# A two-layer graph attention kernel: in the first gather, product 1 is copied from one PSUM bank to another and product 2 is added onto the copy

## The chip, the cores and the metric

The kernel runs on one core of one Trainium2 chip. The metric is the device time of one execution in microseconds; lower is better. A core has five engines with their own instruction queues: TensorE (PE, matmuls), VectorE (DVE), ScalarE (ACT), GpSimd (POOL) and SyncE (SP, which here issues DMAs). Each works through its queue in order and waits for others by semaphores. Matmuls write to PSUM, which has eight banks; ACT and DVE read them out.

## What is computed

Layer norm and ReLU on x (32 batches of 512 nodes by 512 features), then two graph attention layers, then x is added back. Cut to its core:

```
h = relu(layernorm(x))
def gat_layer(x, mask, W, a_src, a_dst, bias, concat):
    xl = (x @ W).reshape(B, N, H, F)
    e = leaky_relu(asrc[:, :, None, :] + adst[:, None, :, :], 0.2)
    e = where(mask, e, -1e9)
    attn = softmax(e, axis=1)
    out = einsum('bsdh,bshf->bdhf', attn, xl)    # the gather
    ...
h = elu(gat_layer(h, mask, W1, ..., concat=True))     # 4 heads of 256 features
h = gat_layer(h, mask, W2, ..., concat=False)         # 1 head of 512
return x + h
```

The gather of the first layer is, for each batch and each of four heads, a product of a 512 x 512 attention matrix `p` with a 512 x 256 block of `xl`, in fp32.

## The kernel before

**Work.** Each batch goes through these stages: loads, norm and transposes (`load`, `norm`, `norm_turn`), masks (`masks`), the first projection (`project1`), the attention weights of four heads (`Soft.first`, `Soft.second`), the first gather (`gather1`), elu (`elu`), the second projection (`project2`), weights of the single head, and the second gather (`gather2`), after which the output is stored. The main loop (L1698) interleaves the stages of batches i, i+1 and i+2: gather of heads 0 and 1 of batch i+1, first half of the projection of batch i+2, gather of heads 2 and 3, the rest of the projection, second gather of batch i, second projection of batch i+1. The first batch is done with plain products (`gather1_plain`, four tiles at a time), before the loop.

**Seven products.** Nearly all matrix products are done as 2 x 2 blocks with Strassen-Winograd's seven block products instead of eight. For this, DVE first makes sums of blocks: for the gather, `sums1` (L1380) makes s1, s2, s4 from `xl` (tile `hs`) and t1, t2 from `p` (tiles `t`), and changes one block of each in place. `BLOCK` (L1152) says to which block of the result each product first goes, and `ACC` (L1154) in which PSUM bank of the unit it is summed: products 1, 6, 7, 4 share bank "a" one after another, 5 and 3 share "b", and 2 has "g" for itself. The result's blocks come from partial sums: block (0,0) is 1 + 2, block (0,1) is 1 + 6 + 5 + 3, and so on. After each product the bank is read out: products 1, 4, 5 and 6 by ACT (`activation`, Identity with scale -1 and the bias), which writes a block of `h1` (tile `h` in the profile), products 2, 7 and 3 by DVE, which subtracts the bank from the block that is already in `h1`. So block (0,0) is written by ACT from product 1 and then changed by DVE with product 2. Product 6 is added by PE onto bank "a" after product 1 has been read out. After products 3 and 4, `elu` (L1343) runs on the half that is then complete: an exponential on ACT (`xr<-h`), then one operation on DVE (`h<-xr,h`).

**Order of the gather.** `PAIRS_OF` (L1428) gives the order of PE's products for two heads at a time: 1, 2, 6, 5, 7, 3, 4, each for the first head and then for the second. The gather of the last batch has an order of its own, `SINGLY` (L1431). Product 5 needs s1 and t1, product 6 needs s2 and t2, products 1, 2, 4 and 7 need blocks of `p` and `xl`.

**Banks.** `Banks` (L46) hands out the eight PSUM banks at build time, first in, first out. With `kept`, `take` gives only a bank that some matmul has written at least that wide, and returns None when there is none; this is for banks that ACT fills and PE then adds onto (`start=False`). The second projection (`sevens`, with a bias `b_sb`) and a small product of the first batch's successor (`forked` in `project1`) do this already: `mm<-b_sb` and `mm<-mm` in the profile.

**What sets the order.** Every operation is entered in a list of jobs (`Program.add`) with a cost and the keys it reads and writes. PE's order is the order of entry. For the other four engines a planner (`Program.order` at L375, `better` at L440, `Run`) simulates the whole program with these costs, looks for places where PE would wait, and changes priorities until it finds fewer. So when a cost, an order or a dependency changes anywhere, the order of DVE, ACT, POOL and SP can change everywhere, from the first instruction on. One job of `gather1` is one product: two matmuls of 128 x 256, each of which is two records in the trace.

All ACT operations of the kernel have line L646 in the profile, all DVE operations L649, most SP DMAs L652, the POOL DMAs L657 and all matmuls L663, since helpers record them; the tiles tell them apart: `mm` are the PSUM banks, `p` the attention weights, `l` the logits on their way to the softmax denominators, `ht` the transposed input, `hs` and `t` the sums of blocks, `stats` the norm's statistics.

Of the kernel before, what the change touches and what calls it, by code (L numbers as in the profile page):

```python
# [15 lines left out]
AF = mybir.ActivationFunctionType  # L16
# [496 lines left out]
def tile_gat(  # L513
# [55 lines left out]
    def tiles(name, n, shape, dtype=F32, pool=sbuf):  # L569
        return [pool.tile(shape, dtype, name=f"{name}{i}") for i in range(n)]  # L570
# [49 lines left out]
    banks = Banks(tiles("mm", 8, [P, 512], F32, psum))  # L620
# [18 lines left out]
    def give_p(pk):  # L639
        if pk[0] == "p":  # L640
            ps_.give(pk)
# [3 lines left out]
    def act(cost, reads, writes, *a, **k):  # L645
        prog.add("ACT", cost, reads, writes, lambda: nc.scalar.activation(*a, **k))  # L646

    def dve(cost, reads, writes, f, *a, **k):
        prog.add("DVE", cost, reads, writes, lambda: f(*a, **k))  # L649
# [10 lines left out]
    def pe(reads, writes, n, calls):  # L660
        def emit():
            for f, a, k in calls:
                f(*a, **k)  # L663

        prog.add("PE", n, reads, writes, emit)
# [440 lines left out]
    M = N // 2  # L1106
# [236 lines left out]
    def elu(g):  # L1343

        keys = [("h1", g, r) for r in range(2)]
        ek, e = xrs.take()
        act(0.62, keys, [ek], e, h1[:, g, :], AF.Exp, bias=-1.0)
        dve(
            0.65, [*keys, ek], keys, nc.vector.scalar_tensor_tensor,
            h1[:, g, :], e, 1.0, h1[:, g, :], op0=OP.min, op1=OP.max,  # L1350
        )
        xrs.give(ek)
# [27 lines left out]
    def sums1(h, pk, p, apart):  # L1380


        def a_block(i, j):
            return (
                xl[:, 2 * j : 2 * j + 2, h, 2 + i * P : 2 + (i + 1) * P],
                [("xl", 2 * j + k, h, i) for k in range(2)],
            )

        def b_block(r, c):
            return (  # L1390
                p[:, 2 * r : 2 * r + 2, c * M : (c + 1) * M], p_keys(pk, (2 * r, 2 * r + 1), (c,))
            )

        a11, a12, a21, a22 = (a_block(i, j) for i in range(2) for j in range(2))
        b11, b12, b21, b22 = (b_block(r, c) for r in range(2) for c in range(2))
        k = KQ + h % 2
        s1, s2 = (
            (hs[:, i, k, :].rearrange("p (k f) -> p k f", f=P), [("hs", i, k)]) for i in range(2)
        )
        s4 = s2  # L1400
        if apart:
            s4 = (hs4[:, h % 2, :].rearrange("p (k f) -> p k f", f=P), [("hs", 2, h % 2)])
        t1, t2 = (
            (t.rearrange("p (k f) -> p k f", f=M), [q]) for q, t in (ts_.take() for _ in range(2))
        )

        def op(cost, f, to, u, v):
            dve(cost, u[1] + v[1], to[1], f, to[0], u[0], v[0])

        add, sub = nc.vector.tensor_add, nc.vector.tensor_sub  # L1410
        op(0.34, add, s1, a21, a22)
        op(0.59, sub, t1, b12, b11)
        op(0.34, sub, s2, s1, a11)
        op(0.59, sub, t2, b22, t1)
        op(0.34, sub, a21, a11, a21)
        op(0.59, sub, b12, b22, b12)
        if apart:
            op(0.34, sub, s4, a12, s2)
        return (
            {1: a11, 2: a12, 3: s4, 4: a22, 5: s1, 6: s2, 7: a21},  # L1420
            {1: b11, 2: b21, 3: b22, 4: b21, 5: t1, 6: t2, 7: b12},
            lambda: op(0.59, sub, b21, b21, t2),
            (lambda: None) if apart else (lambda: op(0.34, sub, s4, a12, s2)),
        )
# [1 line left out]


    PAIRS_OF = tuple(  # L1428
        tuple((h + i, n) for n in (1, 2, 6, 5, 7, 3, 4) for i in range(2)) for h in (0, 2)
    )  # L1430
    SINGLY = (  # L1431
        (0, 1), (0, 5), (0, 2), (0, 6), (0, 3), (1, 1), (0, 7), (1, 5), (1, 2), (0, 4), (1, 6), (1, 3),
        (2, 1), (1, 7), (2, 5), (2, 2), (1, 4), (2, 6), (2, 3), (3, 1), (2, 7), (3, 5), (3, 2), (2, 4),
        (3, 6), (3, 3), (3, 7), (3, 4),
    )

    def gather1(soft, order):

        blocks, bank = {}, {}
        ahead = {h for h, n in order[:2]}  # L1440
        for h in sorted(ahead):
            blocks[h] = sums1(h, *soft.p[h], order is SINGLY)
        for h, n in order:
            if h not in blocks:
                blocks[h] = sums1(h, *soft.p[h], order is SINGLY)
            left, right, late, fourth = blocks[h]
            if n == 4:
                late()
            acc = ACC[n]
            first = n in (1, 2, 5)  # L1450
            if first:
                bank[h, acc] = banks.take(M)
            bk, bt = bank[h, acc]
            ps = bt[:, :M]
            (a, akeys), (w, wkeys) = left[n], right[n]
            pe(
                akeys + wkeys, [bk], KQ * M / 593,
                [
                    (mm, (ps, a[:, k, :], w[:, k, :]),
                     dict(start=(first and k == 0), stop=(k == KQ - 1), skip_group_check=True))  # L1460
                    for k in range(KQ)
                ],
            )
            if n == 6:
                fourth()
            r, c = BLOCK[n - 1]
            g = h * FPH + r
            to, key = h1[:, g, c * M : (c + 1) * M], ("h1", g, c)
            if n in (1, 4, 5, 6):
                act(  # L1470
                    COPY, [bk, "b1"], [key], to, ps, AF.Identity, bias=b1_sb[:, g : g + 1], scale=-1.0,
                )
            else:
                dve(ADD, [bk, key], [key], nc.vector.tensor_sub, to, to, ps)
            if n in (2, 3, 4):
                banks.give(bk)
            if n in (5, 6):
                ts_.give(right[n][1][0])

            if n in (3, 4):  # L1480
                elu(g)
            if n == 4:
                give_p(soft.p.pop(h)[0])
                yield h
# [213 lines left out]
    for i in range(B - 1):  # L1698
# [3 lines left out]
        if last:  # L1702
            for h in gather1(s, SINGLY):
                if h < 2:
                    s.second(h + 2)
                if h == 0:
                    S2[i] = second_layer(i)
                if h == 2:
                    S2[i].second(0)
        else:  # L1710
            run(gather1_plain(s, (0, 1)) if i < PLAIN else gather1(s, PAIRS_OF[0]))
            s.second(2)
            s.second(3)
            S2[i] = second_layer(i)
            S2[i].second(0)
        if front:
# [6 lines left out]
            n = S1[i + 2] = Soft(i + 2, 1, scores_1)  # L1723
# [3 lines left out]
        if not last:  # L1727
            run(gather1_plain(s, (2, 3)) if i < PLAIN else gather1(s, PAIRS_OF[1]))
# [68 lines left out]
```

## Time and profile before

| what | value |
|---|---|
| median of 3 runs | 2760.99 us (2758.34 to 2761.75) |
| the profiled execution | 2761.27 us, its span 2759.5 us |
| mean granted PE clock | 0.999 |
| ACT busy, of the span | 81%, 4751 records |
| POOL busy, of the span | 12%, 356 records |
| DMA | 502.10 MB, mean 182 GB/s |

The span runs from the first to the last instruction on the core; the execution's own time is 1.8 us longer. A profile line of a group reads: line, engine, operation, output tile <- input tiles, shapes, count, then busy us in total, mean ns of one, then the idle time of the engine just before these instructions and what ended it. Durations of instructions that follow each other on one engine overlap: a DVE operation of 128 x 256 has a duration of 0.42 us, and the next one starts some 0.33 us after it. In timelines the columns are start (us from the span's start), duration, engine, line, operation, tiles, shapes and count; consecutive alike instructions are merged. In the table of stretches the columns are the stretch, its length, then busy time and count of PE, PE's weight loads, DVE, ACT and POOL, the granted PE clock, the DMA share and GB/s.

### The profile page before, as it was taken

To read this page: it belongs to the slowest core of one execution; us is meant where nothing else is said; L and a number is where in the kernel's file an instruction comes from. 1 tells how busy PE (TensorE), PEld (TensorE's weight loads), DVE (VectorE), ACT (ScalarE), POOL (GpSimd) and SP (SyncE) were. 2 spreads that over 40 slices of the span, in tenths; PEclk is the share of its full clock that TensorE was granted. 3 is DMA by queue.
4 is the path that set the end of the run, shared out by engine and by line. 5 is a ranking of instruction groups with operands and counts; after the bars stand their busy time and mean duration, and the time that the engine had idled before them with its cause. 6 is when DMAs were issued, how large, how long until landed. Compare 5 with 4: busy or idle time off the path is not lost.

```text
span 2759.5 us, 41946 instructions
## 1 busy us (share of the span) xinstructions
PE 2735.3 (99%) x12490; PEld 2365.6 (86%) x12490; DVE 2627.4 (95%) x6864; ACT 2244.0 (81%) x4751; POOL 323.8 (12%) x356
## 2 busy tenths in 40 slices
PE   7999999999999999999999999999999999999999
PEld 6688888888888888888888888888888888888887
DVE  8999999999999999999999999999999999999996
ACT  5978788888888788887889888888888898888883
POOL 0110111101111011101011110111111110101110
PEclk9999999999999999999999999999999999999999
DMA  8657766667666676776786667767667776668663
GB/s 233 176 153 181 206 178 172 182 179 202 180 184 178 177 184 188 187 183 169 187 204 184 172 178 191 190 184 188 171 180 181 200 189 165 181 183 210 165 172 107
DMA packets 375862, 502.10 MB, mean 182 GB/s; under 512 B 222804, under 2 KB 227668, under 8 KB 375636
## 3 DMA queue, kind: packets, MB, share of 16 engines
q1 hardware_dynamic: 329844, 332.68, 43.7%
q0 software_dynamic: 45792, 166.74, 24.8%
q8 instruction: 101, 1.65, 0.2%
q14 instruction: 125, 1.02, 0.1%
HBM read 316.41 MB, written 51.31 MB: 133 GB/s over the span
## 4 chain that ended last, share of the span: by engine, by line
PE 92%; DVE 3%; DMA 2%; ACT 2%; issue 1%; SPq 0%; DVEq 0%; ACTq 0%
PE mm L663 92%; ACT l L646 1%; DVE p L649 1%; DMA as<-das 0%; DMA adj<-in_adj_dram 0%; DVE h L649 0%; DMA rr<-drr 0%; DVE hs L649 0%; DMA p<-dm 0%; DVE w_sb L649 0%; ACT p L646 0%; DVE l L649 0%; DVE xr L649 0%; DVE t L649 0%; ACT xl L646 0%
## 5 line engine op out<-in xcount | busy, mean ns | idle before, releaser
L663 PE MATMUL mm<-w_sb,hs 128*128 128x257 f32 (+2 forms) x3032 | 697.5, 381 | 5.1 <-DVE hs L649 4.5
L663 PEld LDWEIGHTS mm<-w_sb,hs 128*128 128x128 f32 x3032 | 575.5, 190 | 91.4 <-DVE hs L649 6.1
L657 POOL DMA_DIRECT2D p<-dm x314 | 275.6, 887 | 2261.3 <-DVE p L649 1081.8
L646 ACT ACTIVATE l<-l,low 128x512 f32<-128x512 f32 x640 | 457.4, 717 | 16.0 <-DVE low L649 14.7
L663 PE MATMUL mm<-w_sb,h 128*128 128x257 f32 x2056 | 468.1, 379 | 0.7 <-ACT xl L646 0.7
L663 PE MATMUL mm<-p,xl 128*128 128x256 f32 (+1 forms) x1984 | 465.7, 382 | 0.0
L649 DVE SCALAR_TENSOR_TENSOR p<-rr,z 128x512 f32<-128x512 f32 (+1 forms) x636 | 454.7, 745 | 0.6 <-DMA rr<-drr 0.5
L646 ACT ACTIVATE l<-as,z 128x512 f32<-128x512 f32 x640 | 438.4, 714 | 17.2 <-DMA as<-das 16.6
L663 PEld LDWEIGHTS mm<-w_sb,h 128*128 128x128 f32 x2056 | 389.2, 189 | 59.1 <-ACT xl L646 1.1
L649 DVE CUSTOM_DVE_ANT_1 l<-l,mt 128x512 f32<-128x512 f32 x640 | 427.0, 686 | 7.3 <-ACT l L646 6.4
L663 PEld LDWEIGHTS mm<-p,xl 128*128 128x128 f32 x1984 | 376.8, 190 | 58.6 <-issue 6.9
L646 ACT ACTIVATE p<-p,z 128x512 f32<-128x512 f32 (+1 forms) x636 | 419.0, 716 | 9.6 <-DVE p L649 8.4
L663 PE MATMUL mm<-w_sb,ht 128*128 128x258 f32 x1802 | 421.3, 382 | 3.0 <-DVE xl L649 2.3
L646 ACT ACTIVATE h<-mm,b_sb 128x256 f32<-128x256 f32 (+1 forms) x504 | 232.3, 474 | 204.1 <-PE mm L663 201.8
L663 PEld LDWEIGHTS mm<-w_sb,ht 128*128 128x128 f32 x1802 | 340.1, 190 | 58.6 <-DVE xl L649 7.8
L646 ACT ACTIVATE xl<-mm 128x258 f32<-128x258 f32 (+2 forms) x686 | 253.4, 379 | 96.5 <-PE mm L663 93.3
L649 DVE TENSOR_TENSOR xl<-xl,mm 128x258 f32<-128x258 f32 (+1 forms) x526 | 215.4, 421 | 34.0 <-PE mm L663 29.0
L663 PE MATMUL mm<-t,hs 128*128 128x256 f32 x992 | 225.2, 379 | 0.0
L663 PEld LDWEIGHTS mm<-t,hs 128*128 128x128 f32 x992 | 188.5, 190 | 25.6
L646 ACT ACTIVATE xr<-h 128x512 f32<-128x512 f32 x256 | 158.4, 627 | 53.6 <-DVE h L649 52.6
L649 DVE TENSOR_TENSOR t<-mm,t 128x256 f32<-128x256 f32 (+1 forms) x424 | 172.3, 420 | 13.3 <-PE mm L663 11.9
L663 PE MATMUL mm<-xl,p 128*128 128x256 f32 (+1 forms) x752 | 179.4, 387 | 0.0
(132 smaller groups left out, 3475.1 us busy)
## 6 DMA issues: line engine op xcount, KB each, us to landing
p<-dm POOLq DMA_DIRECT2D x314, 512.0 KB, 5.9
rr<-drr SPq DMA_DIRECT2D x159, 512.0 KB
x<-in_x_dram SPq DMA_DIRECT2D x129, 256.0 KB
adj<-in_adj_dram SPq DMA_DIRECT2D x128, 256.0 KB
as<-das SPq DMA_DIRECT2D x64, 512.0 KB
t<-in_x_dram SPq DMA_DIRECT2D x124, 256.0 KB
out_dram<-t SPq DMA_DIRECT2D x124, 256.0 KB
dm<-m SPq DMA_DIRECT2D x64, 256.0 KB
```

The source lines that it names most:

```text
L646: prog.add("ACT", cost, reads, writes, lambda: nc.scalar.activation(*a, **k))
L649: prog.add("DVE", cost, reads, writes, lambda: f(*a, **k))
L657: lambda: nc.gpsimd.dma_start(to, at, accum_op=OP.add), size,
L663: f(*a, **k)
```

## The change

In `gather1`, for all batches but the first and the last (30 batches, 4 heads, 120 times), product 1 is no longer written to `h1`. ACT copies it from bank "a" to a bank taken for it, which becomes bank "g" (`fork`, a plain Copy). Product 2 is then accumulated by PE onto this copy (`start=False`), and the sum of both is written to `h1` by one ACT operation with scale and bias. The DVE subtraction of product 2 is gone. The order of the products becomes 1, 5, 6, 2, 7, 3, 4. The last batch's gather (`SINGLY`) is as before. If no bank can be had, the old way is taken.

```diff
     PAIRS_OF = tuple(
-        tuple((h + i, n) for n in (1, 2, 6, 5, 7, 3, 4) for i in range(2)) for h in (0, 2)
+        tuple((h + i, n) for n in (1, 5, 6, 2, 7, 3, 4) for i in range(2)) for h in (0, 2)
     )
...
             acc = ACC[n]
-            first = n in (1, 2, 5)
+            first = n in (1, 5) or n == 2 and (h, "g") not in bank
             if first:
                 bank[h, acc] = banks.take(M)
...
             to, key = h1[:, g, c * M : (c + 1) * M], ("h1", g, c)
-            if n in (1, 4, 5, 6):
+            fork = banks.take(M, M) if n == 1 and order is not SINGLY else None
+            if fork:
+                bank[h, "g"] = fork
+                act(0.29, [bk], [fork[0]], fork[1][:, :M], ps, AF.Copy)
+            elif n in (1, 4, 5, 6) or n == 2 and not first:
                 act(
                     COPY, [bk, "b1"], [key], to, ps, AF.Identity, bias=b1_sb[:, g : g + 1], scale=-1.0,
                 )
```

## The prediction

> **What bounds the kernel now.** I read the engine totals first, then the chain that ended last.
>
> ```profile
> PE 2735.3 (99%) x12490; PEld 2365.6 (86%) x12490; DVE 2627.4 (95%) x6864; ACT 2244.0 (81%) x4751; POOL 323.8 (12%) x356
> PE 92%; DVE 3%; DMA 2%; ACT 2%; issue 1%; SPq 0%; DVEq 0%; ACTq 0%
> ```
>
> TensorE (PE) is busy for 2735.3 of 2759.5 us and is 92% of the chain. VectorE (DVE) comes close behind, ScalarE (ACT) has room. The change takes DVE work away, so the first question is how much PE ever waits. The waits of PE:
>
> ```profile
> PE mm L663 <- ACT x L646: 10.6, 2, 10.3
> PE mm L663 <- DVE hs L649: 4.8, 3, 4.3
> PE mm L663 <- DVE xl L649: 2.3, 3, 1.3
> PE mm L663 <- ACT xl L646: 1.2, 2, 0.7
> ```
>
> Columns: total us, times, longest. 10.3 us are the first load and norm, before any matmul; 4.3 are one wait near 48 us. Then busy time by stretch (span and PE's busy time stand first):
>
> ```profile
> 100.00:2600.00 2500.00, 2497.19 (x11481) 2174.38 (x11480) 2404.97 (x6198) 2077.09 (x4392) 298.48 (x323) 1.00 0.69 182
> 2600.00:2700.00 100.00, 97.98 (x448) 84.10 (x447) 96.77 (x234) 82.37 (x179) 12.10 (x14) 1.00 0.61 164
> ```
>
> The 60 changed gathers lie between 135 and 2633 us, all but the last before 2606. From 100 to 2600 us PE idles 2500 - 2497.19 = 2.8 us. So in its own place the change cannot win much more than 2.8 us, 0.1%, whatever it does for DVE.
>
> **The change, part by part.** Counted in the two programs as built: PE has 6261 matmuls in both, SP and POOL the same numbers of instructions, so no DMA is added or removed. DVE loses 120 subtractions `h<-h,mm`; ACT gains 120 copies `mm<-mm` (30 batches x 4 heads). The rows:
>
> ```profile
> L649 DVE TENSOR_TENSOR h<-h,mm 128x256 f32<-128x256 f32 x372 | 151.5, 419 | 1.8 <-PE mm L663 0.5
> L646 ACT ACTIVATE h<-mm,b_sb 128x256 f32<-128x256 f32 x496 | 227.0, 471 | 202.6 <-PE mm L663 200.3 <-DVE hs L649 0.8 <-DVE h L649 0.4
> L646 ACT ACTIVATE mm<-mm 128x258 f32<-128x258 f32 x1 | 0.4, 364 | 0.0
> ```
>
> DVE: 120 x 0.419 = 50.3 us less busy time, 2627 to 2577 (93%). ACT: product 1's drain with bias (0.471) turns into a copy, and product 2 gets the drain instead, so the net addition is one copy: 120 x 0.364 = 43.7 us, 2244 to 2288 (83%). Both lie beside PE, so on the path they are 0. Without cover each would show only as a PE wait. PE's matmuls are the same in number and shape; a product added onto a copied bank is a matmul like any other here: 0.
>
> *The order 1, 5, 6, 2 in place of 1, 2, 6, 5.* Product 5 moves up two places (four matmul records, 0.86 us, per product of a head). One gather in the PE timeline:
>
> ```profile
> 1008.99 3.62 PE L663 MATMUL mm<-p,xl 128*128 128x256 f32 x16
> 1012.45 3.62 PE L663 MATMUL mm<-t,hs 128*128 128x256 f32 x16
> ```
>
> The first line is products 1, 1', 2, 2' (the prime is the second head), the second 6, 6', 5, 5'. Product 5 will start at about 1010.72. Its operand t1 is
>
> ```profile
> 1007.68 1.29 DVE L649 TENSOR_TENSOR t<-p 128x512 f32<-128x512 f32 x2
> ```
>
> done at 1008.97, 1.75 us before. I took the same difference, moved start less end of t1, in all 60 gathers: the smallest is 0.60 us, the next 1.43. Product 6 starts when it did. Cost 0. If DVE ran 0.6 us later there, the first PE wait would appear.
>
> *The copy and the banks.* In the same gather product 1 ends at 1009.9, and ACT drains the two at
>
> ```profile
> 1010.36 1.04 ACT L646 ACTIVATE h<-mm,b_sb 128x256 f32<-128x256 f32 x2
> ```
>
> Behind the copy on ACT stand the drains of 5 and 6. Over the 60 gathers ACT starts that first drain 0.20 to 1.78 us after product 1 ends; product 6, which overwrites the bank, comes three products (2.6 us) after, and product 2, which needs the copy, five. Worst case 1.78 + 0.47 = 2.25 of 2.6: 0.35 us to spare. Bank g is now taken at product 1, by ACT. Going through takes and gives in program order, the bank that the copy gets has had at least eight products (7 us) since its last matmul; no PE product gets a bank sooner than before. I take 0; a wait of one copy at every gather would be 60 x 0.364 = 22 us, the upper end; below, -2.8 us, all the idle time of that stretch.
>
> [...]
>
> *What moves elsewhere.* The planner orders every engine but PE anew, from the start. So I compared the built orders where PE waits most, at 48 us, in the second batch's projection, before any gather of the changed kind.
>
> ```profile
> 45.75 2.67 PE L663 MATMUL mm<-w_sb,ht 128*128 128x258 f32 x10 [0.42 <-ACT ht L646]
> 52.71 1.71 PE L663 MATMUL mm<-w_sb,hs 128*128 128x258 f32 x5 [4.29 <-DVE hs L649]
> ```
>
> ```profile
> 46.80 0.69 DVE L649 CUSTOM_DVE_ANT_1 l<-l,mt 128x512 f32<-128x512 f32 x1
> ...
> 50.14 0.69 DVE L649 BATCH_NORM_STATS2 stats<-x 128x6 f32<-128x512 f32 x1 [0.90 <-DMA x<-in_x_dram]
> ...
> 51.97 0.69 DVE L649 TENSOR_TENSOR hs<-ht 128x512 f32<-128x512 f32 x1
> ```
>
> PE needs the sum `hs<-ht`, which starts at 51.97. In the changed program 13 of DVE's instructions that stood ahead of it come after it, and none comes in: three `l<-l,mt` (0.61 apart: 1.83), one batch statistic (0.61) with its 0.90 wait for a DMA, two `hl` (0.41), and four small ones (`low`, `low`, `rr`, `z`: 0.45); the other three are accumulator reads, inside the 0.61. That is 4.2 us, so the sum could start at 47.8. It also needs ACT's four copies `ht<-mm`: the last now runs at 49.79 to 50.37 after other ACT work, in the changed order the four stand in a row; the first was at 45.12, one `xl<-mm` (0.27) now stands ahead, and at 0.47 apart the last ends at 45.39 + 3 x 0.47 + 0.58 = 47.4. So the sum ends near 48.5, where PE's earlier work ends (48.42). The wait of 4.29 shrinks to about 0.3: -4.0 (bounds -4.3 and 0).
>
> The long wait has a second price. In these stretches the granted clock is the third number from the right:
>
> ```profile
> 48.00:53.00 5.00, 0.71 (x3) 0.30 (x3) 4.10 (x15) 5.00 (x14) 0.00 (x0) 1.00 0.89 276
> 53.00:57.00 4.00, 4.00 (x12) 3.18 (x12) 3.60 (x9) 1.27 (x6) 0.00 (x0) 0.57 0.73 231
> ```
>
> After the 4.29 us wait the clock falls to 0.57 over 4 us: (1 - 0.57) x 4 = 1.7 us lost. After the wait of 1.3 us near 2617 it stays 1.00. A wait of 0.3 is below both: -1.7 (bounds -1.7 and 0). [...]
>
> Next late after that: the first plain gather at 83.61, at 77.9 by this sum, whose four `p` exponentials end by 79.0; PE takes the four 0.86 apart, the third at 79.6, so even unmoved they are in time. I give back 0.5 there (bounds 0 and 5.7, all of it). For the middle and end, where the planner's new order makes new small waits as likely as it ends old ones, I take +0.5 (bounds -4.8, the 2.8 and 2.0 us of idle in the two stretches, and the 22 above).
>
> **Sum.** The profiled execution took 2761.27 us (span 2759.5), 0.3 above the median of 2760.99. 2761.27 - 4.0 - 1.7 + 0.5 + 0.5 = 2756.6.
>
> **Rivals.** (1) *The start's gain is given back.* The gathers at 84 to 111 us depend on DMAs and exponentials that do not start earlier; PE waits there instead, and the time is the present one, 2761. For it: DVE is 96% busy from 50 to 100 us. Against: PE has no wait there now, and `p` is early.
> (2) *DVE's relief removes the small waits too.* Waits on DVE `xl` and `h` near 2617 and in the middle go: another -4.8 at most, about 2752.5. For it: 50 us off DVE. Against: the waits are few, each has its own cause, half are on ACT, which gets more work.
> (3) *Slower: the copy is late on ACT.* The place is product 6 of each pair, which overwrites the bank that the copy reads. It decides once ACT's delay passes 2.6 - 0.47 = 2.1 us, against 1.78 now. At 0.1 to 0.36 us in 60 gathers it costs 6 to 22 us; with the start's gain of 5.7 it must pass 11 us to show. Mid value 15: 2761 - 5 + 15 = 2771. For it: the 0.35 us to spare, and the long `ht` and `adj` operations (1.36 and 1.05 us) on ACT. Against: most delays are 0.2 to 0.6.
> (4) The copy may not be made at all, if no bank is free: excluded, all 120 are in the built program.
>
> **How the numbers follow.** 0.2%, 5.5 us, is about what a measurement can tell from no change: faster is below 2755.5, slower above 2766.5. The forecast, 2756.6, has 0.55 with its own range 2753.5 to 2759.5, so that 0.20 of it lies below 2755.5. Rival 1 has 0.18 (same), rival 2 0.15 (faster), rival 3 0.12 (slower). Faster 0.20 + 0.15 = 0.35; same 0.35 + 0.18 = 0.53; slower 0.12. The range 2750.5 to 2766 takes in all but rival 3 and little below.
>
> **What would show it.** Right: PE's wait on `hs` near 48 us under 1 us and a clock of 1.00 at 49 to 57; DVE near 2577 and ACT near 2288 us busy; PE idle from 100 to 2600 still 2 to 5 us. Wrong: PE waits on ACT `mm` or DVE `t` in the gathers, a new wait at 78 to 111 us, or the 4.3 us wait still there.

## The result and the profile after

| | before | changed |
|---|---|---|
| median of 12 runs, same chip | 2761.47 us (2758.34 to 2765.27) | 2754.11 us (2751.30 to 2760.62) |
| the profiled execution | 2761.27 us | 2758.68 us, its span 2756.9 us |

The ratio is 0.9975 [0.9968, 0.9983]: by it 6.9 us less, 0.25% (the medians differ by 7.4). The profiled execution of the changed kernel is the second longest of its twelve. Its mean granted clock is 0.999, as in three of the twelve (2756.95 to 2760.62 us); the nine with a clock of 1.000 took 2751.30 to 2754.69. Its trace has two stretches of 3.413 us at half clock, 3.4 us lost. So the profile explains only 2.6 of the 6.9 us, and a reader who had this page alone would judge the change too low.

The engine totals and the chain that ended last, changed kernel:

```profile
PE 2732.9 (99%) x12490; PEld 2367.0 (86%) x12490; DVE 2595.0 (94%) x6744; ACT 2281.9 (83%) x4871; POOL 326.5 (12%) x356
PE 97%; DMA 1%; ACT 1%; DVE 0%; SPq 0%; issue 0%; ACTq 0%
```

DVE has 120 records fewer, ACT 120 more, PE the same. The chain now runs through PE for 97% in place of 92%, and DVE's 3% are gone from it. The waits of PE (total us, times, longest):

```profile
PE mm L663 <- ACT x L646: 12.6, 1, 12.6
PE mm L663 <- ACT ht L646: 2.9, 1, 2.9
PE mm L663 <- ACT w_sb L646: 1.9, 1, 1.9
PE mm L663 <- ACT xl L646: 1.6, 1, 1.6
PE mm L663 <- DVE h L649: 0.6, 1, 0.6
PE mm L663 <- DVE hs L649: 0.5, 1, 0.5
```

No line names ACT `mm`, the copy, or DVE `t`, the operand of the product that was moved forward. The wait of 4.3 us on `hs` near 48 us is gone (the 0.5 lies at 656 us), but one of 2.9 on ACT's `ht` stands in its place, and the first line is 2 us longer. The stretches:

```profile
48.00:53.00 5.00, 4.08 (x12) 3.18 (x13) 5.00 (x17) 4.61 (x12) 0.00 (x0) 0.72 0.91 220
53.00:57.00 4.00, 4.00 (x18) 3.39 (x18) 4.00 (x13) 3.51 (x10) 0.00 (x0) 0.92 0.80 281
100.00:2600.00 2500.00, 2497.83 (x11497) 2178.53 (x11496) 2378.79 (x6096) 2120.33 (x4517) 301.53 (x325) 1.00 0.69 183
2600.00:2700.00 100.00, 97.53 (x438) 83.60 (x438) 95.19 (x228) 80.23 (x182) 10.38 (x12) 0.98 0.56 151
```

In this execution the clock still falls, only earlier: (1 - 0.72) x 5 + (1 - 0.92) x 4 = 1.7 us, the very amount that was to go. From 100 to 2600 us PE idles 2.2 us. A gather of the changed kind, first on PE, then on ACT:

```profile
1007.80 1.89 PE L663 MATMUL mm<-p,xl 128*128 128x256 f32 x8
1009.53 3.62 PE L663 MATMUL mm<-t,hs 128*128 128x256 f32 x16
```

```profile
1008.87 0.37 ACT L646 ACTIVATE mm<-mm 128x256 f32<-128x256 f32 x1 [0.29 <-PE mm L663]
...
1009.73 0.37 ACT L646 ACTIVATE mm<-mm 128x256 f32<-128x256 f32 x1
```

Products 1, 1', then 5, 5', 6, 6' without a pause; the first copy ends at 1009.24, the second at 1010.10, and product 6 starts at about 1009.53 + 1.73 = 1011.26. That is 2.0 us after the first copy.

**Why the start gained less in this execution.** The first matmul before, then the first matmuls of the changed kernel and those near 48 us:

```profile
10.29 1.11 PE L663 MATMUL mm<-identf,x 128*128 128x128 f32 x4 [10.29 <-ACT x L646]
```

```profile
12.65 3.84 PE L663 MATMUL mm<-identf,x 128*128 128x128 f32 x16 [12.65 <-ACT x L646]
...
48.92 3.63 PE L663 MATMUL mm<-w_sb,ht 128*128 128x258 f32 x10 [2.85 <-ACT ht L646]
52.35 2.55 PE L663 MATMUL mm<-w_sb,hs 128*128 128x258 f32 x8
```

The first matmul runs 2.36 us later. On DVE, before and then changed:

```profile
9.23 0.16 DVE L649 SCALAR_TENSOR_TENSOR stats<-stats 128x4 f32<-128x4 f32 x1
```

```profile
7.67 0.69 DVE L649 BATCH_NORM_STATS2 stats<-x 128x6 f32<-128x512 f32 x1 [1.19 <-DMA x<-in_x_dram]
...
11.23 0.42 DVE L649 SCALAR_TENSOR_TENSOR xr<-w_sb,p 128x256 f32<-128x256 f32 x1 [2.32 <-DMA p<-in_L_gnn_att_src_dram]
11.58 0.08 DVE L649 DVE_READ_ACCUMULATOR xr<-w_sb,p 128x1 f32 x1
11.58 0.16 DVE L649 SCALAR_TENSOR_TENSOR stats<-stats 128x4 f32<-128x4 f32 x1
```

The last line is the norm's shift, which ACT needs for the first normalized `x` (it starts at 11.78). Nothing in it needs the load of the attention vectors, but on DVE's queue it now stands behind a product that waits 2.32 us for that load; before, it ran at 9.23. That is not all of the 2.36 us: the fourth load of `x` is now issued behind one of the weights, the last batch statistic waits for it (the first line), and the step of the norm on POOL, which the shift needs, ends at 9.91 in place of 8.20. So the product accounts for at most 11.58 - 9.91 = 1.7 us.

The wait of 2.85 us on `ht` has another cause. On ACT the four copies `ht<-mm` stand behind work that waits for the load `as<-das`:

```profile
41.80 0.72 ACT L646 ACTIVATE l<-as,z 128x512 f32<-128x512 f32 x1 [5.75 <-DMA as<-das]
...
48.30 2.04 ACT L646 ACTIVATE ht<-mm 128x512 f32<-128x512 f32 x4
```

Three experiments below, e1, e6 and e7, have the changed kernel's order on DVE, ACT, POOL and SP up to 118 us. Their first matmuls are as late (13.15, 12.65 and 13.02 us), but this operation of ACT waited only 2.56, 2.19 and 2.33 us, the copies started at 46.80, 46.70 and 45.92, and PE did not wait for `ht`. So the late first matmul comes with the order in every execution that was profiled, and the late `ht` does not. Why the load was late in this one is open.

PE has the same matmuls in both programs, in the same order but for the places within the changed gathers. So I compared them by lead: when PE starts its k-th matmul record in one profiled execution and in the other, and how the difference grows. Positive is earlier than before.

| kernel | to 118 us | 118-640 | 640-680 | 680-2640 | 2640-end | sum |
|---|---|---|---|---|---|---|
| changed | 1.6 | 1.7 | -2.7 | 5.6 | -3.6 | 2.5 |
| e8, changed, first 13 us in the old order | 5.9 | 1.4 | 0 | 4.1 | -1.5 | 9.9 |
| e6, changed, each copy twice | 3.9 | 0.8 | -0.3 | -1.8 | -2.0 | 0.5 |
| e7, changed, one more DVE read per copy | 4.7 | -4.9 | -1.1 | -20.0 | -6.6 | -27.9 |
| e11, changed, other seed | 0.6 | 1.7 | 0 | 5.1 | -2.5 | 4.9 |
| e12, changed, other seed | -0.6 | 1.7 | -9.3 | 2.2 | -2.7 | -8.7 |
| e2, changed, start in the old order | 2.2 | 1.7 | -8.0 | 2.5 | -3.6 | -5.3 |
| e4, copy alone | 4.3 | 1.4 | 0 | -13.2 | -2.0 | -9.5 |
| e3, order alone | 3.1 | 0.7 | 0 | -0.9 | -4.3 | -1.5 |
| e5, subtractions left out | -0.1 | 0.6 | 0 | 0.1 | -0.8 | -0.2 |
| e1, old with the new start | 3.7 | -5.7 | 0 | -0.7 | -1.6 | -4.2 |
| e9, e10, old, other seeds | 3.3, 0.6 | 0.2, 0.2 | 0, 0 | 1.2, 1.2 | -0.7, -3.2 | 3.9, -1.2 |

The changed kernel wins in two places: a little at the start, more in the long middle, where the forecast saw nothing; it loses some at 640 us and at the end. At the start, e1, e6 and e7 have the same order and lead by 3.7 to 4.7 us in place of 1.6. At the end, the wait of 1.92 us on `w_sb` near 2674 us and 1.7 us of half clock after it (3.413 us at 0.5) make up the 3.6.

The 5.6 us from 680 to 2640 us are more than PE's idle time there before, 3.3 us. A matmul record lasts 0.38 us here and the next starts 0.217 us after it, so the first 0.16 us of a wait lie under the record before and do not count as idle. Taken from the starts instead (each step from one start to the next, less 0.217 us, where that is over 0.012), the waits of this stretch add up to 6.0 us before and 0.7 in the changed kernel.

### The profile page after: what moved, and what is told of

Same layout as the page of the kernel before. It is cut to its first block, busy times and chain, and to the rows that moved or that the text cites. A ratio compares the mean times of both kernels' runs of the same rounds, so it can differ in the third digit from the quotient of the medians.

```text
span 2756.9 us, 41901 instructions
## 1 busy us (share of the span) xinstructions
PE 2732.9 (99%) x12490; PEld 2367.0 (86%) x12490; DVE 2595.0 (94%) x6744; ACT 2281.9 (83%) x4871; POOL 326.5 (12%) x356
## 4 chain that ended last, share of the span: by engine, by line
PE 97%; DMA 1%; ACT 1%; DVE 0%; SPq 0%; issue 0%; ACTq 0%
PE mm L663 97%; DMA x<-adj 0%; DMA w_sb<-dm 0%; ACT l L646 0%; DMA w_sb<-in_L_gnn_W_dram 0%; DMA as<-das 0%; DMA das<-as 0%; SPq L652 0%; DVE h L649 0%; ACT x L646 0%; DVE hs L649 0%; ACT ht L646 0%; DVE w_sb L649 0%; ACT w_sb L646 0%; DVE xl L649 0%
## 5 line engine op out<-in xcount | busy, mean ns | idle before, releaser
L646 ACT ACTIVATE h<-mm,b_sb 128x256 f32<-128x256 f32 (+1 forms) x504 | 226.2, 475 | 184.5 <-PE mm L663 183.8
```

## The experiments

Theory A: the gain is the start (the wait on `hs` and the half clock); the middle is a wash. Rival B: the DVE time that the subtractions free ends the small waits of the middle. Rival C: neither; any new plan of the planner lands some us up or down, and this one landed well. Each ratio stands against runs of the kernel before on the same chip; times in us by a ratio are (ratio - 1) x 2762.

**e1, e2: the start alone, and all but the start.** The first operations are issued in the other program's order, the rest in the program's own: 610 operations for e1 (on the kernel before), 499 for e2 (on the changed one).

```diff
+    FIXED = (91, 0, 411, 1, 2, 11, ...)
...
-        for j in self.order():
+        taken = set(self.FIXED)
+        for j in (*self.FIXED, *(j for j in self.order() if j not in taken)):
```

> The kernel before, with nothing of the change but the order in which the engines issue their first 610 operations (up to the first changed gather, about 130 us), which is taken from the changed kernel; what follows keeps the order of before. If the gain comes from the new order of the start: 3 to 6 us faster than before (ratio 0.998 to 0.999). If it comes from the freed DVE time in the gathers: within 1.5 us of before. If it is spread over many places of the planner's new order: 1 to 3 us faster.

Measured: 2762.82 us, ratio 0.9999 [0.9990, 1.0008]: nothing. The clock was 1.000 in all its runs, and the profile has a lead of 3.7 us at 118, yet 5.7 are lost by 640, 4.0 of them by 250:

```profile
136.49 3.72 PE L697 MATMUL mm<-t,hs 128*128 128x256 f32 x16 [0.81 <-ACT h L680]
...
145.16 2.06 PE L697 MATMUL mm<-p,xl 128*128 128x256 f32 x8 [1.12 <-DVE h L683]
```

These are waits in the first gathers, where the new start meets the old order, with work in the wrong place for it. So a start is not a part that can be taken over by itself: most of the gain was given back, at 120 to 250 us rather than at 84 to 111.

> The changed kernel, with the first 499 operations (up to the first changed gather) in the order of before. If the gain comes from the start: back to 2760 to 2762 us. If it comes from the gathers and what follows them: it stays at 2753 to 2756. The lead of the changed kernel over before, read matmul by matmul, grows by about 3 us between 150 and 2640 us in the profiled runs, so a mix would give 2757 to 2759.

Measured: 2757.59, ratio 0.9986 [0.9977, 0.9995]: -3.9 us without the new start. The difference to the changed kernel (0.0011, 3.0 us) is what the new start is worth here, with an uncertainty as large. Nor need all of the 3.9 us lie behind the start: in the profiled execution the wait near 48 us is 3.49 us, no half clock follows it (1.00 from 48 to 57 us), and the lead at 118 us is 2.2 us with the old order; the other executions have no trace. The profiled execution was an outlier of 2766.49: at 657 us PE waits 5.3 on `hs`, because of

```profile
658.22 1.34 ACT L674 ACTIVATE ht<-x 128x1024 uint16<-128x1024 uint16 x1 [8.10 <-DMA x<-adj]
```

a transposing load that ACT had to wait 8.10 us for. Theory A, that the middle is a wash, is weakened by e2 but not refuted by it: 1.7 us would be left if all its executions led by 2.2 us at 118. The same trace has, at one of the 60 gathers, what rival 3 of the prediction feared, PE first and then ACT:

```profile
1922.34 1.13 PE L691 MATMUL mm<-t,hs 128*128 128x256 f32 x4 [1.14 <-ACT mm L674]
```

```profile
1920.08 1.06 ACT L674 ACTIVATE adj<-x 128x1024 uint16<-128x1024 uint16 x1 [1.12 <-DMA x<-adj]
...
1921.92 0.37 ACT L674 ACTIVATE mm<-mm 128x256 f32<-128x256 f32 x1
```

The copy stands on ACT behind an `adj` operation that waits for a transposing load, and product 6 waits 1.14 us for the copy. e8 lost 0.27 us in the same way at the same gather.

**e3, e4: the order alone, and the copy alone.**

```diff
# e3, on the kernel before; e4 is the changed kernel with the opposite edit
-        tuple((h + i, n) for n in (1, 2, 6, 5, 7, 3, 4) for i in range(2)) for h in (0, 2)
+        tuple((h + i, n) for n in (1, 5, 6, 2, 7, 3, 4) for i in range(2)) for h in (0, 2)
```

> Only the order of products 1, 5, 6, 2, 7, 3, 4; product 2 is still subtracted by DVE. If the freed DVE time matters: no gain, 2759 to 2763 us. If any new order that the planner makes is worth a few us either way: anything from 2753 to 2768. No wait of PE on the sums t or hs in the gathers under either theory.

Measured: 2763.05, ratio 1.0003 [0.9995, 1.0012]. The order alone costs and brings nothing, in the one plan that was made for it.

> Only the copy from bank to bank, with the products in the order 1, 2, 6, 5, 7, 3, 4 of before. [...] If the order was changed to give the copy time: PE waits on ACT mm in most gathers, 0.2 to 1 us each, 10 to 50 us slower, 2770 to 2810. If the copy hides anyway: 2753 to 2757.

Measured: 2768.88, ratio 1.0020 [1.0012, 1.0029], 5.5 us slower; the loss that I expected was larger and in another place. No line of PE's waits names ACT `mm`: neither product 2, which follows product 1 by one product of the other head here (0.86 us), nor product 6 waits for it. PE waits on `hs`, the input sums of the projection, 7.7 us in four waits from 100 to 2600, such as

```profile
1079.33 2.70 PE L663 MATMUL mm<-w_sb,hs 128*128 128x258 f32 x8 [2.08 <-DVE hs L649]
```

So with DVE relieved just as much, this plan is worse. The relief does not bring a gain by itself. Whether the loss is the plan's or the product order's is not shown: e4 was not run with another seed.

**e5: the DVE time alone.** The kernel before in its own order, with 120 subtractions not issued. It leaves out product 2 in block (0,0) of these gathers; PE still computes it.

```diff
-                dve(ADD, [bk, key], [key], nc.vector.tensor_sub, to, to, ps)
+                skip = n == 2 and order is not SINGLY
+                dve(ADD, [bk, key], [key], (lambda *a: None) if skip else nc.vector.tensor_sub, to, to, ps)
```

> The kernel before in its own order on every engine, but the 120 subtractions of product 2 on DVE are not issued, so block (0,0) lacks product 2. This is the freed DVE time by itself, without a new order and without the copies. If DVE's relief is what the change brings: 3 to 7 us faster than before, as the new order with the old start was (ratio 0.9986). If the order is what matters and the freed DVE time only leaves DVE idle: within 1.5 us of before.

Measured: 2762.25, ratio 1.0000 [0.9991, 1.0009]. DVE is down to 2598.1 us busy, and PE's small waits stay:

```profile
118.00:2640.00 2522.00, 2518.52 (x11603) 2197.60 (x11602) 2399.73 (x6149) 2093.52 (x4435) 302.02 (x327) 1.00 0.69 182
```

PE idles 3.5 us there, before it was 4.1. Freed time in an order that was made without it was worth nothing here. Rival B falls in its plain form.

**e6, e7: work put back into the changed kernel's order.** e6 does every copy twice; e7 adds one DVE read of product 2's bank, into a tile that nobody uses, after each drain of product 2.

```diff
# e6
-                act(0.29, [bk], [fork[0]], fork[1][:, :M], ps, AF.Copy)
+                copy = (fork[1][:, :M], ps, AF.Copy)
+                prog.add("ACT", 0.29, [bk], [fork[0]],
+                    lambda copy=copy: [nc.scalar.activation(*copy) for _ in range(2)])
# e7, in the drain of product 2
+                    nc.vector.tensor_scalar_mul(junk, drain[1], -1.0)
```

> The changed kernel in its own order, each copy from bank to bank done twice (120 more ACT operations, 44 us of ACT time). If ACT has the room and the copy has slack: within 1.5 us of the changed kernel, 2752.5 to 2756. If ACT is close to its limit in the gathers (rival 3 of the prediction): PE waits on ACT mm, 6 to 30 us slower.

> The changed kernel in its own order, with one more DVE operation per copy: DVE reads product 2's bank once more (128 x 256) into an unused tile, next to ACT's drain. DVE's load is then that of before. If DVE's relief brings the gain: 3 to 5 us of it are lost, 2757 to 2760. If the order brings it and DVE has slack: 2753 to 2756.

Measured: e6 2760.95, ratio 0.9991 [0.9982, 1.0000], so 120 unplanned copies on ACT cost 4.4 us by the ratios (6.8 by the medians). e7: 2788.93, ratio 1.0092 [1.0079, 1.0106], so 120 unplanned operations on DVE cost 32 us by the ratios (35 by the medians). In e7 DVE is 2626.6 us busy, as in the kernel before, but

```profile
PE mm L664 <- DVE xl L650: 10.8, 29, 0.8
```

29 waits where the kernel before had three. Its lead falls steadily, by 20 us between 680 and 2640. The added reads also stand behind ACT's drain of product 2: DVE sat idle 12.7 us, 34 times, for it, so e7 puts back a new wait for ACT along with the time, and the two are not told apart. The time that was freed could not be put back at that place. That each order is fitted to its own load would explain both e5 and e7; it is argued, since no work was added to the order of before.

**e8: the first 13 us.** The changed kernel with its first 49 operations in the old order (the same edit as e2, a shorter list).

> The changed kernel, with only the first 49 operations (loads, norm and first transposes, up to about 13 us) in the order of before. In the profiled runs the first matmul came 2.4 us later with the new order, since a step of the norm stands behind an operation that waits for a load. If that is a steady loss: 2 us faster than the changed kernel, 2751 to 2753. If later waits absorb it: 2753 to 2756.

Measured: 2751.27 us (2749.01 to 2757.54, 5 runs), ratio 0.9960 [0.9948, 0.9973]: 11 us under the kernel before, and the best of all; its interval still touches that of the changed kernel.

```profile
10.55 1.11 PE L669 MATMUL mm<-identf,x 128*128 128x128 f32 x4 [10.55 <-ACT x L652]
...
45.24 2.55 PE L669 MATMUL mm<-w_sb,ht 128*128 128x258 f32 x10 [0.82 <-ACT ht L652]
47.96 2.01 PE L669 MATMUL mm<-w_sb,hs 128*128 128x258 f32 x8 [0.17 <-DVE hs L655]
```

```profile
48.00:53.00 5.00, 5.00 (x23) 4.39 (x24) 5.00 (x16) 4.62 (x14) 0.00 (x0) 1.00 0.86 308
...
118.00:2640.00 2522.00, 2521.44 (x11624) 2202.23 (x11623) 2402.22 (x6170) 2138.27 (x4566) 304.42 (x328) 1.00 0.70 183
```

The first matmul is back at 10.55, the sum `hs` is there 0.17 us late, `ht` 0.82, the clock is 1.00. This is the start as the forecast had it. The lead is 6.4 us at 57 and 5.9 at 118. From 118 to 2640 PE idles 0.6 us.

**e9 to e12: the planner's luck.** The planner's random search gets another seed; nothing else changes.

```diff
-        chance = Random(1)
+        chance = Random(2)    # e9 on the kernel before, e11 on the changed one; Random(3) for e10, e12
```

> The kernel before, with another seed of the planner's random tries, so another order of DVE, ACT, POOL and SP for the same work. If the planner's luck decides: its time lies anywhere in 2752 to 2770, and overlaps with that of the changed kernel under other seeds. If the freed DVE time lets the planner find better orders: 2759 to 2768, above both changed kernels under other seeds.

> As the run before, a third seed. Luck: 2752 to 2770. Freed DVE time: 2759 to 2768.

> The changed kernel with the second seed. Luck: 2752 to 2770, overlapping with the two of before. Freed DVE time: 2750 to 2758, below both kernels of before under the same seeds.

> The changed kernel with the third seed. Luck: 2752 to 2770. Freed DVE time: 2750 to 2758.

| plan | before | changed |
|---|---|---|
| seed 1 | 1 | 0.9975 [0.9968, 0.9983] |
| seed 2 | 0.9989 [0.9980, 0.9998] | 0.9988 [0.9979, 0.9996] |
| seed 3 | 0.9995 [0.9987, 1.0004] | 1.0014 [1.0002, 1.0027] |
| mean | 0.9995 | 0.9992 |

The changed plans spread over 0.0039, 11 us; the means differ by 0.0002 before they are rounded, under 1 us. With three plans each, the edit cannot be told from no edit; what was measured as a gain is this edit *with this plan*. Yet the middle, but for 640 to 680 us, points the same way in all the changed plans. e11, where nothing is late at 640 us:

```profile
118.00:2640.00 2522.00, 2521.94 (x11631) 2203.68 (x11630) 2405.02 (x6169) 2144.13 (x4573) 304.68 (x327) 1.00 0.69 183
```

0.06 us of idle in 2522. In e12, ACT waited again for a transposing load, and PE, through DVE's `hs`, for ACT:

```profile
661.95 1.34 ACT L646 ACTIVATE ht<-x 128x1024 uint16<-128x1024 uint16 x1 [8.99 <-DMA x<-adj]
```

Of e12's 9.3 us lost there, 6.2 are one wait of PE on `hs`. The mean clock of this execution is 0.998, against 0.999 in that of the kernel before, so some of the rest may be half clock; where it lay was not shown.

## Why the prediction was right, and where it was not

Faster it was, by 6.9 us where 4.4 were forecast against the median (2756.6 to 2760.99); the changed median, 2754.11, lies in the range and in the forecast's own range (2753.5 to 2759.5), below the 2755.5 under which I had put 0.35. That it came so near is luck in part. Two terms were off, in opposite directions, and no term stands for the plan: with seed 3 the same edit gave 2764.83, above the kernel before.

- *DVE and ACT beside PE: 0.* Right in time. The rows say ACT 2281.9 us (forecast 2288). DVE is at 2595, not 2577. The group of the subtractions did lose its 50 us, 151.5 to 101.7:

```profile
L649 DVE TENSOR_TENSOR h<-h,mm 128x256 f32<-128x256 f32 x252 | 101.7, 412 | 2.2 <-PE mm L663 1.7
L646 ACT ACTIVATE mm<-mm 128x256 f32<-128x256 f32 x120 | 44.4, 374 | 10.7 <-PE mm L663 8.7 <-DVE z L649 0.5 <-DVE t L649 0.5
```

  But records on DVE overlap, and the engine's busy time counts a moment under two records once: it fell by 32.4 us here and by 29.3 in e5, 0.24 to 0.27 for each of the 120 in place of 0.419, about what is left of 0.42 when 0.09 at each end is shared with a neighbour. I took a duration where a share of busy time was asked for.
- *The order 1, 5, 6, 2: 0.* Right: e3 gives 1.0003, and no wait of PE names `t` in the changed kernel.
- *The copy and the banks: 0.* Right for the changed kernel's profile, where no wait names the copy, and for e4's. But the 0.35 us to spare were not always there: in e2 product 6 waited 1.14 us and in e8 0.27 for the copy, each at one gather of 60. That is rival 3's mechanism and place, behind the `adj` operation that it names, at far less than its price. Even a doubled copy costs 4 to 7 us in 120 (e6), far from the 22 us of a wait of one copy at each gather. The edit holds four banks longer, "b" and "g" of each head; "a" is held from product 1 to product 4 as before.
- *The wait on `hs` and the half clock: -5.7, with 0.5 given back.* Right as a mechanism, and in its size, when the first 13 us are as before: e8 has 6.4 us at 57 and 5.9 at 118. In the changed kernel itself it was too high, because I compared the orders only where PE waited and took the time before 45 us as unchanged. There the new order costs 2.36 us at the first matmul. With it, the lead at 118 us is 3.7, 3.9 and 4.7 us in e1, e6 and e7, which have this start, 3.0 by e2 against the changed kernel, and 1.6 in its own profiled execution, where the late `as<-das` added 2.85 us of waiting and a half clock. That nine of the twelve runs had a mean clock of 1.000 (of the kernel before, 8 of 91 in the experiments) fits the half clock gone in most runs, but not in the one that was profiled.
- *The middle and end: +0.5.* This term was mis-sized: by e2 it is -3.9 us at most, and in the profiled execution the lead grows by 5.6 from 680 to 2640, against -2.7 at 640 and -3.6 at the end. The small waits of the middle did go, as rival 2 had it. That the change "cannot win much more than 2.8 us" in its own place was wrong: PE's idle time leaves out what lies under the matmul records, and by the starts the waits from 118 to 2640 us were 7.8 us before and 3.5 in the changed kernel. But rival 2's reason is not enough for it: e5 shows that the relief does nothing in the old order, e4 that it can come with a worse one, and e7 fits a new order that needs it.
- *Rival 1, the start's gain given back,* happened in e1, where the new start was joined to the old order, though later than it says and not at 84 to 111 us.

Of the rival theories, C is the one the runs leave standing for the total: the plans of one program differ by as much as the change brought. What may go beyond luck is the middle: between 118 and 2640 us PE waits 2.1 us in the changed kernel, 0.6 in e8 and 0 in e11, against 4.1, 2.7 and 2.4 in the three old plans (9.8 in e12 and 6.9 in e2, most of it at 640), and all five kernels with copy and new order and no work added lead by 2 to 6 us between 680 and 2640 (e9 and e10, the other old plans, by 1.2). But these are three plans only, e12's is among them with the largest loss at 640, and e8 and e2 share theirs with the changed kernel. Open: whether better middles come with this edit in general (e4's does not), why the transposing load near 640 us lands late in some plans or runs, and why these plans wait more at the end (1.5 to 3.6 us).

## What to carry to other kernels

When queues are ordered by a planner, an edit buys a new plan for the whole program: re-seed the planner on both sides before a gain of a few tenths of a per cent is credited to the edit. Time freed on an engine that is not the bottleneck is worth what the order makes of it: nothing in the old order here. Work added to an order that was planned without it can cost all that it takes: 32 us for e7's reads, with the wait that they bring. Compare the built orders from the first instruction on, not only where the old trace waited: the order of the first 49 operations came with some 4 us by the ratios (e8 against the changed kernel, intervals overlapping). And one profiled execution is one draw: a wait that is in it can be missing from the next with the same order, as the 2.85 us on `ht` were.

## What the runs showed of the chip

The half clock came in stretches of 3.413 us at 0.5, after some waits of PE and not after others:

| PE waited | until | clock after it |
|---|---|---|
| 4.29 us (before) | 52.71 us | 0.50 from 53.57 to 56.98 us |
| 2.85 us (changed) | 48.92 us | 0.50 from 50.23 to 53.64 us |
| 1.92 us (changed) | 2674.06 us | 0.50 from 2675.08 to 2678.49 us |
| 3.49 us (e2) | 51.73 us | 1.00 from 48 to 57 us |
| 1.65 us (changed) | 662.83 us | 1.00 from 653 to 670 us |
| 1.33 us (before) | 2618.15 us | 1.00 from 2612 to 2630 us |

So the length of a wait alone does not decide it: 1.92 us was followed by half clock, and 3.49 us was not. What decides it was not shown.

A copy of 128 x 256 fp32 from PSUM to PSUM took ACT 0.374 us (mean of 120, changed kernel), 0.1 less than a drain with scale and bias to SBUF (0.472, mean of 496).
